# Layer 0 of a two-layer graph kernel: unnormalised row weights, sums inside the owner product, division on ScalarE

## The chip, the core and the metric

The kernel runs on one core of a Trainium2 chip. The metric is the device time of one execution in microseconds. The profile is one profiled execution of the same program; its span and the median of the timed runs differ a little, and both are given below.

Engines: PE (TensorE) multiplies matrices into PSUM, DVE (VectorE) and ACT (ScalarE) work element by element, POOL (GpSimd) issues the indirect DMAs that gather rows, SP issues most other DMAs. Each engine works through its own queue in the order written.

## The reference

`x` is 4096 x 512, `adj` a 4096 x 4096 integer matrix with about 0.1% ones. Layer 0 is graph attention with 8 heads of 64; layer 1 averages the neighbours and mixes them with the node's own row. Each layer is added to its input and normalised.

```python
Wh = einsum('nf,hfo->hno', x, W)
f1 = einsum('hno,ho->hn', Wh, a[:, :F_OUT])
f2 = einsum('hno,ho->hn', Wh, a[:, F_OUT:])
e = leaky_relu(f1[:, :, None] + f2[:, None, :], 0.2)
attn = softmax(where(adj > 0, e, NEG_INF), axis=-1)
x = layernorm(x + concat_heads(attn @ Wh))          # layer 0
agg = mask @ x / max(deg, 1)
nb_f, self_f = agg @ W_nb + b_nb, x @ W_self + b_self
x = layernorm(x + relu(concat(self_f, nb_f) @ W_comb + b_comb))   # layer 1
```

## The kernel before

The 4096 nodes are 32 blocks of 128. The kernel keeps no dense matrix: it turns each row of `adj` into a short list of neighbour indices and gathers rows.

*List stage.* Each adjacency half block is loaded (L391), turned to bf16 on ScalarE (L397), folded by small matmuls (L415) into keys, of which DVE takes maxima (L430). Once for every four blocks `decode` (L432, a generator that yields between its pieces; `some(lists)` advances it by one piece) turns the keys into `lst` (up to 16 indices a node). A node's first `K0` = 3 neighbours have slots of their own; further ones go into `KH` = 2 shared slots of 128 rows for the block, each row with an owner. `own` (one byte each) holds for every shared slot the matrix "row r belongs to node c", `of` the transposed form. At the same time node rows `x @ [W | W a]` are computed (L343) and stored as table `t0`, rows of 8 head scores and 512 values. The last four blocks' lists (28 to 31) are decoded after the last load, between 238 and 257 us.

*Layer 0 loop* (L999 to L1061). Iteration i does parts of several blocks: it gathers block i+4, weighs i+2, sums i+1, normalises i and multiplies block i-1 for layer 1. `gather` (L601) issues five indirect DMAs on POOL, one for each slot, into one of five buffers `g`. For block b:

- `a_weights` (L627): scores e = leaky_relu(f2 gathered + f1), 128 x 5 x 8, on DVE; `a_exp` (L634) on ScalarE.
- `a_shared_sum` (L640): owner matrix times the shared slots' exponentials on PE; `a_sum` (L649 to L653) adds the three own slots and takes the reciprocal, on DVE.
- `a_reach` (L659): PE takes the reciprocal to the shared slots with the transposed owner matrix `st`, which ScalarE casts from `of` (L625). `a_normed` (L667, L670) multiplies the exponentials on DVE.
- `a_weigh` (L674) multiplies the gathered rows by the weights, in place; `a_adds` (L696, L698) adds the three own slots; `a_x` (L682) copies x into PSUM on ScalarE and `a_shared` (L686) adds the owner matrix times the shared rows onto it: two matmuls of 512 columns.
- `a_moments` (L702) on DVE adds both parts and takes the row sum; `root` (L709 to L715) and `norm` (L718) on ScalarE normalise; `transposed` (L322 on PE, copy L328 on ScalarE) and `a_z` (L723 on PE, copy L727) make layer 1's neighbour product, stored as table `t1`.

`fold_weights` (L273) multiplies W_nb by W_comb in sixteen matmuls (L281); it runs in the entry to the loop, between the list pieces. `fold_bias` (L297, line L300) adds four DVE instructions in iterations 2 to 5 and 16 to 19, `sum_bias` one product in iteration 20.

*Layer 1* (L1067 to L1141) gathers from `t1`. The first six blocks' gathers are split: early ones (L608) may start before `t1` is complete, in the buffers that layer 0 gives up; late ones (L611) fetch the rest. Per block it runs `g_self` (L755), `g_shared` (L762), moments and norm.

PSUM is one pool with fixed names: `sm` and `nm` and `pw` two banks each, `key` and `tp` one. A wait between instructions is a semaphore; the order of work is the order in the source, since the schedule is manual.

Of the kernel before, what the change touches and what calls it, by code (L numbers as in the profile page):

```python
# [31 lines left out]
F32 = mybir.dt.float32  # L32
# [8 lines left out]
P = 128  # L41
# [16 lines left out]
LE = 26  # L58
LX = 31
G = 4  # L60
FMAX = 30.0
SHIFT = 136 * 512


@with_exitstack
# [25 lines left out]
def listed_layers(  # L91
# [40 lines left out]
    xt = tc.dram_tile([N, FIN], F32, name="xt")  # L132

    const = ctx.enter_context(tc.tile_pool(name="const", bufs=1))
    ps = ctx.enter_context(tc.tile_pool(name="ps", bufs=1, space=PSUM))
    small = ctx.enter_context(tc.tile_pool(name="small", bufs=3))

    nc.scalar.preload_act_table_set("natural_log_exp_and_others")
# [134 lines left out]
    def fold_weights(loaded, place):  # L273

        wr, wc = loaded
        wT = turned(wr, 0, place(0))
        for c in range(FB):
            nxt = turned(wr, c + 1, place(c + 1)) if c + 1 < FB else None
            mp = ps.tile([P, HD], F32, name="tp", bufs=1)
            for d in range(FB):  # L280
                nc.tensor.matmul(  # L281
                    mp, lhsT=wT[:, d, :], rhs=wc[:, d, :], start=(d == 0), stop=(d == FB - 1)
                )
                if d == FB - 1:
                    nc.scalar.copy(wr[:, c, :], mp)  # L285
                yield
            wT = nxt
# [144 lines left out]
    def decode(b0, dp, place):  # L432
# [60 lines left out]
        for g in range(G):  # L493
            for k in range(KH):
# [1 line left out]
                    pe[:, g, k, :], lhsT=sts[g][:, ts(k, P)], rhs=lst[:, b0 + g, K0:],  # L496
                    start=True, stop=True,
                )
        for g in range(G):
            nc.scalar.copy(of[:, b0 + g, :], sts[g])  # L500
        nc.vector.tensor_copy(es[:, bs], pe[:, :, :, 0:EX])
        nc.vector.tensor_copy(f1s[:, bs, K0:KS, :], pe[:, :, :, EX:])
        kx = dp.tile([P, G, KH], F32, name="kx", bufs=1)
# [104 lines left out]
    def gather_early(b, pool):  # L608
        return gather(t1[0 : 2 + min(LE + b, LX) * P, :], b, pool, idxe)
# [2 lines left out]
        rows_of(gl[:, b, :], t1[:, :], idxl[:, b : b + 1])  # L612


    G0, OWN, ST, E, DN, PR, Y, NM, MV, RS = ({} for _ in range(10))

    def a_owners(b, wp):
        OWN[b] = wp.tile([P, KH, P], F32, name="own", bufs=4)
        nc.scalar.copy(
            OWN[b].rearrange("p k c -> p (k c)"), own[:, b].rearrange("p k c -> p (k c)")  # L620
        )

    def a_owned(b, wp):
        ST[b] = wp.tile([P, KH, P], F32, name="st", bufs=2)
        nc.scalar.copy(ST[b].rearrange("p k c -> p (k c)"), of[:, b, :])  # L625

    def a_weights(b, wp):  # L627
        gw = G0[b][:, :, 0:H]
        e = E[b] = wp.tile([P, KS, H], F32, name="e", bufs=3)
        nc.vector.tensor_add(e, gw, f1s[:, b])  # L630
        nc.vector.scalar_tensor_tensor(e, e, SLOPE, e, OP.mult, OP.max)

    def a_exp(b):
        nc.scalar.activation(E[b], E[b], AF.Exp)  # L634

    def a_shared_sum(b):

        DN[b] = ps.tile([P, H], F32, name="sm", bufs=2)
        for k in range(KH):
            nc.tensor.matmul(  # L640
                DN[b], lhsT=OWN[b][:, k, :], rhs=E[b][:, K0 + k, :],
                start=(k == 0), stop=(k == KH - 1),
            )

    def a_sum(b, wp):

        pd = DN[b]
        dn = DN[b] = wp.tile([P, H], F32, name="dn", bufs=2)
        nc.vector.tensor_reduce(  # L649
            dn, E[b][:, 0:K0, :].rearrange("p k h -> p h k"), AX.X, OP.add  # L650
        )
        nc.vector.tensor_add(dn, dn, pd)
        nc.vector.reciprocal(dn, dn)  # L653

    def a_reach(b):

        PR[b] = ps.tile([P, KH, H], F32, name="sm", bufs=2)
        for k in range(KH):
            nc.tensor.matmul(  # L659
                PR[b][:, k, :], lhsT=ST[b][:, k, :], rhs=DN[b], start=True, stop=True  # L660
            )

    def a_normed(b):

        e = E[b]
        w = E[b] = ps.tile([P, KS, H], F32, name="key", bufs=1)
        nc.vector.tensor_tensor(  # L667
            w[:, 0:K0, :], e[:, 0:K0, :], DN[b].unsqueeze(1).to_broadcast([P, K0, H]), OP.mult
        )
        nc.vector.tensor_mul(w[:, K0:KS, :], e[:, K0:KS, :], PR[b])  # L670

    def a_weigh(b, sl, to=None):
        gv = G0[b][:, sl, H:TW].rearrange("p k (h d) -> p k h d", h=H)
        nc.vector.tensor_tensor(  # L674
            gv if to is None else to.rearrange("p (k h d) -> p k h d", k=1, h=H), gv,
            E[b][:, sl].unsqueeze(3).to_broadcast([P, sl.stop - sl.start, H, D]), OP.mult,
        )

    def a_x(b):

        NM[b] = ps.tile([P, HD], F32, name="nm", bufs=2)
        nc.scalar.copy(NM[b], xs[:, b, :])  # L682

    def a_shared(b):
        for k in range(KH):
            nc.tensor.matmul(  # L686
                NM[b], lhsT=OWN[b][:, k, :], rhs=G0[b][:, K0 + k, H:TW],
                start=False, stop=(k == KH - 1), skip_group_check=True,
            )

    def a_adds(b, wp):

        yp = ps.tile([P, HD], F32, name="pw", bufs=2)
        a_weigh(b, slice(0, 1), yp)
        a_weigh(b, slice(1, K0))
        nc.vector.tensor_add(yp, yp, G0[b][:, 1, H:TW])  # L696
        Y[b] = wp.tile([P, HD], F32, name="y", bufs=2)
        nc.vector.tensor_add(Y[b], yp, G0[b][:, 2, H:TW])  # L698

    def a_moments(b):  # L700
        mu = MV[b] = small.tile([P, 1], F32, name="ln_sum")
        nc.vector.scalar_tensor_tensor(  # L702
            Y[b], Y[b], 1.0, NM[b], OP.mult, OP.add, accum_out=mu
        )

    def root(b, wide):
# [88 lines left out]
    def some(todo):  # L795
        for p in todo:
            next(p, None)
# [9 lines left out]

    oo_cm = tc.tile_pool(name="owners", bufs=1, side="right")
    oo = oo_cm.__enter__()
    of = oo.tile([P, NB, KH * P], U8, name="of")  # L810
    own = oo.tile([P, NB, KH, P], U8, name="own8")
    dp_cm = tc.tile_pool(name="decode", bufs=1, side="right")
    dp = dp_cm.__enter__()
# [84 lines left out]
        return wp.tile([P, KH * P], F32, name="own", bufs=4)  # L898

    def on_last(b):  # L900
        if b % 2 == 0:
            last[0] = wp.tile([P, FB, P], F32, name="xT", bufs=2)
        return last[0].rearrange("p (g k) r -> p g (k r)", g=2)[:, b % 2, :]

    last = {}

    def store(w, row, eng=nc.scalar):
        eng.dma_start(t0[2 + w * P : 2 + (w + 1) * P, :], row[:, 0:TW])
# [65 lines left out]
        return wp.tile([P, FW], F32, name="row", bufs=2)[:, 0:FIN]  # L974

    m2s = fold_weights(loaded, place)
    a_owners(0, wp)
    a_owned(0, wq)
    for k in range(7):
        some(lists)  # L980
    for k in range(4):
        next(m2s)
    lists = [decode(NB - G, dp, on_last)]
    for k in range(8):
        some(lists)
    for k in range(3):
        next(m2s)
    for k in range(3):
        some(lists)
    for k in range(2):  # L990
        next(m2s)


    def on(b):
        return 0 <= b < NB

    XT, G1 = {}, {}
    biased = fold_bias(loaded, bcol[:, FB:])
    for i in range(-2, NB + 1):  # L999
        if on(i):  # L1000
            a_moments(i)
        if on(i - 1 + GA):
            G0[i - 1 + GA] = gather(t0, i - 1 + GA, gps[(i - 1 + GA) % GA])
        elif i > 0:
            b = i - 1 + GA - NB
            G1[b] = gather_early(b, gps[(NB + b) % GA])
        if on(i + 1):
            a_reach(i + 1)
        if i == -1:
            for k in range(2):  # L1010
                next(m2s)
        if i >= -1 and on(i + 2):
            a_owned(i + 2, wq)
        if on(i + 1):
            a_x(i + 1)
            a_normed(i + 1)
            a_weigh(i + 1, slice(K0, KS))
        if on(i + 2):
            a_weights(i + 2, wq)
        if on(i):  # L1020
            root(i, xs[:, i, :])
        if on(i + 2):
            a_exp(i + 2)
        for k in range({-2: 3}.get(i, 0)):
            some(lists)
        if on(i):
            norm(i, xs[:, i, :])
        if on(i - 1):
            a_z(i - 1, XT.pop(i - 1), m2, wp)
        if on(i + 1):  # L1030
            a_adds(i + 1, wq)
        if i == 0:
            a_shared_sum(i + 2)
            a_shared(i + 1)
        if on(i):
            XT[i] = transposed(i, wp)
            store_xT(i, XT[i])
        if on(i + 2):
            if i:
                a_shared_sum(i + 2)  # L1040
            for k in range({-2: 1}.get(i, 0)):
                some(lists)
            a_sum(i + 2, wq)
            for k in range({-2: 1}.get(i, 0)):
                some(lists)
        for k in range({-2: 3, -1: 2}.get(i, 0)):
            next(m2s)
        if on(i + 1) and i:
            a_shared(i + 1)
        if on(i + 3):  # L1050
            a_owners(i + 3, wp)
        if 2 <= i < 6:
            next(biased)
        if i == 7:
            loaded = load_fold(0, w_self, m1, weight(fc, "wc"))
        if 16 <= i < 20:
            if i == 16:
                biased = fold_bias(loaded, bcol[:, 0:FB])
            next(biased)
        if i == 20:  # L1060
            sum_bias()  # L1061


    dp_cm.__exit__(None, None, None)
    oo_cm.__exit__(None, None, None)
# [74 lines left out]
            nc.vector.tensor_add(flag, fl[:, 0:1], fl[:, 1:2])  # L1140
    g_norm(NB - 1, wp)  # L1141
    fc_cm.__exit__(None, None, None)


@with_exitstack
# [391 lines left out]
```

## Time and profile before

| | us |
|---|---|
| median of 3 runs (691.61 to 692.17) | 691.87 |
| span of the profiled execution | 691.2 |
| list stage, to the last adjacency load's landing | 0 to 226.4 |
| block 0's normalisation starts (first L709) | 265.03 |
| block 31's normalisation starts | 481.84 |
| last `a_z` copy ends | 490.2 |
| last PE instruction ends | 677.9 |

Busy time by stage, from the windows view (us; the granted TensorE clock as a share of full speed):

| window | length | PE | DVE | ACT | POOL | clock |
|---|---|---|---|---|---|---|
| 228.0 to 262.0, entry | 34.0 | 29.59 | 25.88 | 9.63 | 26.04 | 0.73 |
| 262.0 to 282.4 | 20.4 | 17.68 | 14.23 | 10.66 | 13.63 | 0.75 |
| 282.4 to 317.5 | 35.1 | 34.18 | 32.57 | 24.71 | 23.93 | 1.00 |
| 317.5 to 481.8 | 164.3 | 161.87 | 147.29 | 114.55 | 110.99 | 1.00 |
| 481.8 to 502.0, exit | 20.2 | 17.41 | 7.00 | 8.56 | 15.05 | 1.00 |

How to read it: the busy share of an engine is only meaningful within a stage. "Spacing" below is the distance from the start of one instruction to the start of the next on the same engine; it is less than the duration where instructions overlap, and more where one waits. PEld is the weight load of PE, which overlaps its matmuls. A row such as `L723 x8` stands for four matmuls of float32, of which each leaves two records.

### The profile page before, as it was taken

The page shows a single profiled execution, that of the slowest core. Times are in us where ns is not written, and L with a number is a line of the kernel's source. Part 1 is how long each engine was busy: PE and PEld are TensorE (multiplying, and loading weights), DVE is VectorE, ACT ScalarE, POOL GpSimd, SP SyncE. Part 2 cuts the span into 40 slices and gives each one's busy share as a digit, 9 for nine tenths or more (in the row PEclk, how much of TensorE's full clock was granted, in tenths as well). Part 3 has the DMA queues.
Part 4 walks back from the last instruction along what each step waited for, and adds up shares of the span by engine and source line. Part 5 has one row for each costly group of instructions (what it writes and reads, how often), then busy time and mean ns, then how long its engine had stood idle before and what let it go on. Part 6 is the DMA issues. An engine that isn't in the chain of part 4 may idle for free.

```text
span 691.2 us, 9191 instructions
## 1 busy us (share of the span) xinstructions
PE 626.3 (91%) x2354; PEld 345.0 (50%) x2354; DVE 498.4 (72%) x1431; ACT 455.6 (66%) x1044; POOL 348.0 (50%) x410
## 2 busy tenths in 40 slices
PE   4688998897798698999999999999899999999993
PEld 2466766665565444545455444554344444444441
DVE  6246996998787878799988998898304656666663
ACT  3677988888777434667677767776316567767764
POOL 4001111010011677677676776747776677777760
PEclk9999999999999587999999999999999999999997
DMA  8999999999899877788989888968978889998991
GB/s 259 404 408 408 410 407 408 407 408 409 322 325 334 275 196 214 226 265 270 381 274 282 262 263 265 279 215 272 298 206 268 277 300 308 316 304 298 329 308 70
DMA packets 92038, 209.65 MB, mean 303 GB/s; under 512 B 13694, under 2 KB 13702, under 8 KB 91978
## 3 DMA queue, kind: packets, MB, share of 16 engines
q1 hardware_dynamic: 63024, 114.05, 44.6%
q0 software_dynamic: 28624, 94.39, 43.9%
q10 hardware_dynamic: 330, 0.54, 0.2%
q8 instruction: 21, 0.34, 0.2%
q14 instruction: 39, 0.32, 0.1%
HBM read 175.25 MB, written 33.69 MB: 302 GB/s over the span
## 4 chain that ended last, share of the span: by engine, by line
PE 60%; DVE 14%; DMA 14%; ACT 4%; issue 4%; POOL 2%; SPq 1%; DVEq 0%; ACTq 0%; POOLq 0%
PE pw L723 12%; DMA at<-in_adj_dram 11%; PE nm L755 8%; PE pw L755 8%; PE nm L686 7%; PE pw L343 5%; PE nm L762 4%; PE pw L762 4%; PE tp L281 3%; ACT ab L397 3%; POOL g L592 2%; PE tp L322 2%; PE sm L659 2%; DMA g<-t,idx 2%; PE sm L640 1%
## 5 line engine op out<-in xcount | busy, mean ns | idle before, releaser
L592 POOL DMA_INDIRECT g<-t,idx x290 | 280.6, 968 | 116.4 <-issue 49.7
L397 ACT ACTIVATE ab<-at 128x2048 bf16<-128x2048 int32 x64 | 122.2, 1913 | 33.3 <-DMA at<-in_adj_dram 28.0
L343 PE MATMUL pw<-w_sb,xT 128*128 128x264 f32 x512 | 133.3, 407 | 10.7 <-DVE sums L332 4.7
L723 PE MATMUL pw<-wr,xT 128*128 128x512 f32 x256 | 119.7, 611 | 1.4 <-ACT xT L328 1.3
L343 PEld LDWEIGHTS pw<-w_sb,xT 128*128 128x128 f32 x512 | 96.2, 197 | 39.6 <-issue 7.3
L354 POOL COPY f1s<-lst 128x24 f32<-128x24 f32 x32 | 7.3, 229 | 180.8 <-DVE fmax L351 96.4
L674 DVE TENSOR_TENSOR g<-g,key 128x1024 f32<-128x1024 f32 x64 | 77.8, 1216 | 1.1
L723 PEld LDWEIGHTS pw<-wr,xT 128*128 128x128 f32 x256 | 47.0, 194 | 49.3 <-issue 47.5
L686 PE MATMUL nm<-g,own 128*128 128x512 f32 x128 | 64.5, 627 | 0.0
L755 PE MATMUL nm<-m,xT 128*128 128x512 f32 x128 | 57.5, 592 | 0.0
L755 PE MATMUL pw<-m,xT 128*128 128x512 f32 x128 | 57.5, 592 | 0.0
L778 DVE SCALAR_TENSOR_TENSOR sm<-y,lst,nm 128x512 f32<-128x512 f32 x16 | 12.1, 755 | 52.8 <-PE nm L772 29.2
L709 ACT ACTIVATE xs<-y,ln_sum 128x512 f32<-128x512 f32 x32 | 23.1, 722 | 39.2 <-DVE y L702 39.2
L322 PEld LDWEIGHTS tp<-ident,xs 128*128 128x128 f32 x256 | 30.2, 147 | 36.3 <-ACT xs L718 18.4
L322 PE MATMUL tp<-ident,xs 128*128 128x128 f32 x256 | 41.7, 287 | 7.4 <-DVE sums L332 7.1
L347 DVE COPY row<-pw 128x264 f32<-128x264 f32 x64 | 26.9, 422 | 19.4 <-PE pw L343 14.6
L755 PEld LDWEIGHTS pw<-m,xT 128*128 128x128 f32 x128 | 24.3, 190 | 30.6 <-issue 30.4
L755 PEld LDWEIGHTS nm<-m,xT 128*128 128x128 f32 x128 | 24.3, 190 | 30.6 <-issue 30.6
L592 POOL DMA_INDIRECT g<-t,idxe x30 | 28.4, 947 | 16.8 <-issue 6.7
L281 PE MATMUL tp<-wc,row 128*128 128x512 f32 x64 | 34.1, 676 | 2.0 <-ACT m L285 1.2
L762 PE MATMUL nm<-g,own 128*128 128x512 f32 x64 | 30.2, 594 | 1.2 <-ACT nm L746 1.2
L686 PEld LDWEIGHTS nm<-g,own 128*128 128x128 f32 x128 | 22.5, 196 | 16.3 <-issue 15.9
(213 smaller groups left out, 1072.8 us busy)
## 6 DMA issues: line engine op xcount, KB each, us to landing
at<-in_adj_dram SPq DMA_DIRECT2D x64, 1024.0 KB, 10.7
xt<-xT SPq DMA_DIRECT2D x32, 256.0 KB, 4.1
t<-row SPq DMA_DIRECT2D x32, 256.0 KB, 3.9
xT<-xt SPq DMA_DIRECT2D x32, 256.0 KB, 4.9
out_dram<-row SPq DMA_DIRECT2D x32, 256.0 KB, 5.2
t<-row POOLq DMA_DIRECT2D x31, 260.0 KB, 5.5
xs<-in_x_dram SPq DMA_DIRECT2D x31, 256.0 KB, 10.9
g<-t,idx POOLq DMA_INDIRECT x290, 4.8
```

The lines of the kernel that those rows point to most:

```text
L281: nc.tensor.matmul(mp, lhsT=wT[:, d, :], rhs=wc[:, d, :], start=(d == 0), stop=(d == FB - 1))
L322: nc.tensor.transpose(tp[:, c, :], xs[:, b, ts(c, P)], ident)
L343: nc.tensor.matmul(pw, lhsT=xT[:, c, :], rhs=w_sb[:, c, k * HW : (k + 1) * HW], start=(c == 0), stop=(c == FB - 1),)
L347: nc.vector.tensor_copy(row[:, k * HW : (k + 1) * HW], pw)
L397: nc.scalar.activation(ab, loads.pop((b, h)), AF.Relu, accum_out=asum[:, b, h : h + 1])
L592: nc.gpsimd.indirect_dma_start(out=out, out_offset=None, in_=table, in_offset=bass.IndirectOffsetOnAxis(ap=at, axis=0),)
L674: nc.vector.tensor_tensor(gv if to is None else to.rearrange("p (k h d) -> p k h d", k=1, h=H), gv, E[b][:, sl].unsqueeze(3).to_broadcast( ...
L686: nc.tensor.matmul(NM[b], lhsT=OWN[b][:, k, :], rhs=G0[b][:, K0 + k, H:TW], start=False, stop=(k == KH - 1), skip_group_check=True,)
L709: nc.scalar.activation(wide, Y[b], AF.Square, bias=MV[b], scale=-float(HD), accum_out=rs)
L723: nc.tensor.matmul(pz, lhsT=xT[:, c, :], rhs=m2[:, c, :], start=(c == 0), stop=(c == FB - 1))
L755: nc.tensor.matmul(NM[b], lhsT=xT[:, c, :], rhs=m1[:, c, :], start=False, stop=(c == FB - 1), skip_group_check=True,)
L762: nc.tensor.matmul(NM[b], lhsT=OWN[b][:, k, :], rhs=g[:, K0 + k, 0:HD], start=False, stop=(k == KH - 1), skip_group_check=True,)
```

## The change

The weights are no longer normalised before they are used. Rows are weighed by plain exponentials; the exponentials of the shared slots are written into the gathered rows, in front of the values (columns 0 to 7), so that the owner product sums weights and values together, and each node's sum is divided out at the end, head by head, by eight ScalarE instructions (`a_scale`). `a_shared_sum`, `a_sum`, `a_reach`, `a_normed`, `a_owned`, `a_x` and the store `of` go. The product for a block, `num`, is 8 sums and 512 values, kept in two banks: 264 columns and 256. The three own slots are weighed and added straight into `num` on DVE before the owner product adds to it; x is added in `a_moments`.

The loop is one step deeper: iteration i weighs i+3, sums i+2, multiplies owners and divides i+1, normalises i. `a_owners` and the gather move ahead accordingly (gather of i+6). Block 2 is gathered before the loop. The last four blocks' lists are decoded one piece an iteration, over iterations -3 to 12; `last` is a buffer of its own for them. PSUM is laid out anew for the loop and again after it (class `Banks`), with four matmuls that fill the two `num` tiles once. `FMAX`, the bound on head scores above which the dense path would be taken, goes from 30 to 20.

```diff
-FMAX = 30.0
+FMAX = 20.0
+class Banks:
+    def stage(self, bufs, names=None):
+        self.close()
+        self.n += 1
+        self.cm = self.tc.tile_pool(name=f"ps{self.n}", bufs=1, space=PSUM)
+        self.pool = self.cm.__enter__()
+        self.bufs, self.names = bufs, names or {}
+    def tile(self, shape, dtype, name, bufs=None):
+        name = self.names.get(name, name)
+        return self.pool.tile(shape, dtype, name=name, bufs=self.bufs[name])
...
-        for g in range(G):
-            nc.scalar.copy(of[:, b0 + g, :], sts[g])
...
     def a_exp(b):
-        nc.scalar.activation(E[b], E[b], AF.Exp)
-    def a_shared_sum(b):
-    def a_sum(b, wp):
-    def a_reach(b):
-    def a_normed(b):
+        e = E[b]
+        w = E[b] = ps.tile([P, KS, H], F32, name="ew")
+        nc.scalar.activation(w, e, AF.Exp)
+        nc.scalar.activation(G0[b][:, K0:KS, 0:H], e[:, K0:KS, :], AF.Exp)
+    def halves_of(t):
+        return t[:, H : H + 2 * (2 * HH - H)].rearrange(
+            "p (a c) -> p a c", a=2
+        )[:, :, 0:HH]
+    def a_first(b):
+        NM[b] = ps.tile([P, 2 * HD], F32, name="num")
+        nc.vector.tensor_tensor(
+            halves_of(NM[b]).rearrange("p a (h d) -> p a h d", d=D),
+            G0[b][:, 0, H:TW].rearrange("p (a h d) -> p a h d", a=2, d=D),
+            E[b][:, 0].rearrange("p (a h) -> p a h", a=2).unsqueeze(3).to_broadcast(
+                [P, 2, H // 2, D]
+            ),
+            OP.mult,
+        )
+    def a_own_sum(b):
+        nc.vector.tensor_reduce(
+            NM[b][:, 0:H], E[b][:, 0:K0, :].rearrange("p k h -> p h k"), AX.X, OP.add
+        )
+    def a_adds(b):
+        for k in range(1, K0):
+            nc.vector.tensor_add(
+                halves_of(NM[b]), halves_of(NM[b]),
+                G0[b][:, k, H:TW].rearrange("p (a c) -> p a c", a=2),
+            )
     def a_shared(b):
-        for k in range(KH):
-            nc.tensor.matmul(
-                NM[b], lhsT=OWN[b][:, k, :], rhs=G0[b][:, K0 + k, H:TW],
-                start=False, stop=(k == KH - 1), skip_group_check=True,
-            )
+        for a in range(2):
+            r = slice(a * (H + HH), H + HH + a * HH)
+            for k in range(KH):
+                nc.tensor.matmul(
+                    NM[b][:, a * HD : a * HD + r.stop - r.start],
+                    lhsT=OWN[b][:, k, :], rhs=G0[b][:, K0 + k, r],
+                    start=False, stop=(k == KH - 1), skip_group_check=True,
+                )
+    def a_recip(b, wp):
+        RD[b] = wp.tile([P, H], F32, name="rd", bufs=2)
+        nc.vector.reciprocal(RD[b], NM[b][:, 0:H])
+    def a_scale(b):
+        Y[b] = ps.tile([P, HD], F32, name="yp")
+        for h in range(H):
+            a, q = divmod(h, H // 2)
+            o = a * HD + (1 - a) * H + q * D
+            nc.scalar.mul(
+                Y[b][:, h * D : (h + 1) * D], NM[b][:, o : o + D], RD[b][:, h : h + 1]
+            )
-    def a_moments(b):
+    def a_moments(b, wp):
+        yp = Y[b]
+        Y[b] = wp.tile([P, HD], F32, name="y", bufs=2)
...
-            Y[b], Y[b], 1.0, NM[b], OP.mult, OP.add, accum_out=mu
+            Y[b], yp, 1.0, xs[:, b, :], OP.mult, OP.add, accum_out=mu
...
+    ps.stage(
+        dict(num=2, ew=1, yp=1, tp=1, pw=1), dict(key="yp", sm="tp", mp="pw")
+    )
+    for k in range(2):
+        t = ps.tile([P, 2 * HD], F32, name="num")
+        for a in range(2):
+            nc.tensor.matmul(
+                t[:, a * HD : (a + 1) * HD], lhsT=triu, rhs=cols, start=True, stop=True
+            )
+    G0[2] = gather(t0, 2, gps[2])
...
-    for i in range(-2, NB + 1):
+    for i in range(-3, NB + 2):
+        if on(i + 1):
+            a_shared(i + 1)
+        if on(i + 1 + GA):
+            G0[i + 1 + GA] = gather(t0, i + 1 + GA, gps[(i + 1 + GA) % GA])
+        elif on(i + GA - NB - 1) and i + GA - NB - 1 < GA:
+            b = i + GA - NB - 1
+            G1[b] = gather_early(b, gps[(NB + b) % GA])
+        if on(i + 3):
+            a_weights(i + 3, wq)
+        if on(i + 2):
+            a_weigh(i + 2, slice(K0, KS))
+        if on(i + 1):
+            a_recip(i + 1, wq)
+        if on(i + 2):
+            a_first(i + 2)
+            a_weigh(i + 2, slice(1, K0))
+            a_own_sum(i + 2)
+            a_adds(i + 2)
+        if on(i):
+            root(i, xs[:, i, :])
+            norm(i, xs[:, i, :])
+        if on(i + 1):
+            a_scale(i + 1)
+        some(lists)
+        if on(i + 1):
+            a_moments(i + 1, wq)
+        if on(i + 3):
+            a_exp(i + 3)
+        for k in range({-3: 3, -2: 2, -1: 2}.get(i, 0)):
+            next(m2s)
+        if on(i + 4) or i == -3:
+            a_owners(i + 4, wp)
+        if on(i - 1):
+            a_z(i - 1, XT.pop(i - 1), m2, wp)
+        if on(i):
+            XT[i] = transposed(i, wp)
+            store_xT(i, XT[i])
...
+    ps.stage(dict(nm=2, pw=2, sm=2, key=1, tp=1), dict(mp="tp"))
```

## The prediction

> **What bounds the kernel now.** The page first, then windows by stage, the chain of waits and the timeline of one iteration. The run has three stages: lists from the adjacency matrix (0 to 226 us), layer 0 (to 490 us), layer 1. Page, windows (length; busy us of PE, PEld, DVE, ACT, POOL, instructions in brackets; granted clock, DMA share, GB/s), chain (start, length), and ScalarE's timeline:
>
> ```profile
> PE 626.3 (91%) x2354; PEld 345.0 (50%) x2354; DVE 498.4 (72%) x1431; ACT 455.6 (66%) x1044; POOL 348.0 (50%) x410
> ...
> 268.00:270.00 2.00, 2.00 (x5) 0.97 (x5) 1.93 (x3) 0.00 (x0) 1.48 (x2) 0.50 0.78 210
> ...
> 317.50:481.80 164.30, 161.87 (x573) 82.80 (x573) 147.29 (x335) 114.55 (x307) 110.99 (x117) 1.00 0.87 277
> ...
> 317.48 3.54 PE pw L723 x8
> 321.80 1.82 PE nm L686 x4
> 323.96 3.54 PE pw L723 x8
> ...
> 282.40 0.72 ACT L709 ACTIVATE xs<-y,ln_sum 128x512 f32<-128x512 f32 x1 [1.16 <-DVE y L702]
> ...
> 330.95 0.72 ACT L709 ACTIVATE xs<-y,ln_sum 128x512 f32<-128x512 f32 x1 [1.21 <-DVE y L702]
> 331.58 0.19 ACT L709 ACTIVATION_READ_ACCUMULATOR xs<-y,ln_sum 128x1 f32 x1
> 331.80 0.29 ACT L712 ACTIVATE ln_rs<-ln_rs,eps 128x1 f32<-128x1 f32 x1
> 332.13 0.20 ACT L713 ACTIVATE ln_rs<-ln_rs 128x1 f32<-128x1 f32 x1
> 332.24 0.19 ACT L714 ACTIVATE ln_sum<-ln_sum 128x1 f32<-128x1 f32 x1
> 332.45 0.29 ACT L715 ACTIVATE ln_sum<-ln_sum,ln_rs 128x1 f32<-128x1 f32 x1
> 332.94 0.24 ACT L634 ACTIVATE e<-e 128x40 f32<-128x40 f32 x1 [0.19 <-DVE e L631]
> 333.08 0.80 ACT L718 ACTIVATE xs<-y,ln_sum,ln_rs 128x512 f32<-128x512 f32 x1
> 334.49 0.58 ACT L727 COPY row<-pw 128x512 f32<-128x512 f32 x1 [0.60 <-PE pw L723]
> 334.97 0.59 ACT L328 COPY xT<-tp 128x512 f32<-128x512 f32 x1
> 335.45 0.42 ACT L619 CAST own<-own 128x256 f32<-128x256 uint8 x1
> 335.75 0.41 ACT L625 CAST st<-of 128x256 f32<-128x256 uint8 x1
> 336.06 0.60 ACT L682 COPY nm<-xs 128x512 f32<-128x512 f32 x1
> ...
> 481.84 0.72 ACT L709 ACTIVATE xs<-y,ln_sum 128x512 f32<-128x512 f32 x1 [1.81 <-DVE y L702]
> ```
>
> The loop's stage has PE at 161.9 of 164.3 us and DVE at 147.3, tied through L653, L659, L670 and L702; ScalarE has 30% free. From block 2's L709 (282.40) to block 31's (481.84) are 199.4 us, 29 steps of 6.88. The 268 line shows half clock in the entry.
>
> **What the Trainium skill says.** "ScalarE: Activation LUTs", section "What ACT_TABLE_LOAD costs": an ACTIVATE with immediates takes 186 ns + 0.833 per element, each per-partition pointer 93 more, neighbours overlap by 93. The trace agrees: 187 ns (L714), 294 with one pointer (L715), 802 for 512 elements with two (L718); L625 starts 0.30 us after a 0.42 us cast. Same page, section "Step-by-step: what each stage is for": ScalarE writes PSUM sooner than SBUF; L736, SBUF to PSUM, is 578 ns where the formula gives 613. "TensorE: Matmul & The Clock Gate", Part 1: half clock after about 3.4 us of idling, until as much sustained work. Here PE idled 2.7 us before L640 at 267.24; then L723 took 5.62 us instead of 3.68.
>
> **The change part by part.** (1) PE, per block. The sums L640 and reaches L659 go: in the chain of waits 0.35 and 0.34 us. The owner product becomes four matmuls of 264 or 256 columns: L343's 264-column form issues eight rows in 1.79 us against L686's 1.82. PE is left with 3.54 (L723) + 0.5 (transposes) + 1.8 = 5.9 us.
>
> (2) DVE, per block. Its spacing without waits is 6.57 us (L670's successor at 324.77 to that at 331.34). L652, L667 and L670 go, 0.20 + 0.29 + 0.22; the other widths stay. About 5.8. The moments now also wait for ScalarE's divisions. Queued behind them are the next weights; from those to the last add I sum starts of the same rows: 0.37 + 1.14 + 0.15 + 0.60 + 1.14 + 0.20 + 0.80 + 0.70 = 5.1.
>
> (3) ScalarE, per block: the cast `st` (0.30 spacing) and copy of x (0.49) go; a second small exp comes (0.12), and eight scalings of 128x64, PSUM to PSUM, by a pointer. The order of instructions shows that seven of them wait on ScalarE itself, so they can't overlap. No row is this operation. From above: 186 + 53 + 93 = 332 ns by the formula, plus 0.03 (end of L712 to L713), 0.37 apart. From below: no wait felt, 0.25 apart. PSUM ends cost less: L335, 128x128 from PSUM, is 273 ns with its accumulator, leaving 166 fixed, and L736 leaves 151. I take 166 - 20 + 53 + 100 = 300 ns, 0.33 apart. Eight, up to the next exp's start: 7 x 0.33 + 0.30 - 0.09 = 2.52.
>
> The iteration by starts, in its new order: square 0.63, read 0.22, Ln 0.33, exp 0.11, mul 0.21, mul 0.32, normalise 0.71, scalings 2.52, exps 0.26, owners 0.30, two copies 0.98: 6.6; the same rows of before add up to 4.74 where the windows show 114.55/164.3 x 6.88 = 4.80, so I add 0.06: 6.65. That makes ScalarE the longest cycle. Does anything stretch it? Take block i's square as 0. Block i+1's divisions run from 2.6 to 5.2; before them stands the new wait for DVE's reciprocal, with both exps, the owners' cast and two copies queued behind it, but the reciprocal follows only weights and the weighing of two rows on DVE (0.37 + 1.14 after the moments) and the owner product of the step before, so it is ready near 0.9. DVE's moments of i+1 take 5.2 to 5.9, ahead of their square at 6.65. DVE's next series ends 5.1 later, at 4.3 of the next cycle, 0.9 before its moments can start; then the owner product runs 4.3 to 6.1. L723 waits for the copy of the transposes, at 0.1, and ends at 3.7, the transposes at 4.2; their copy on ScalarE comes at 6.2. Nothing is late, so 6.65 stands.
>
> (4) POOL. Five gathers a block at 1.25 apart are 6.26 us, below the cycle. Buffers are freed in the order first, add, add, owner product, and refilled three iterations before use: nothing.
>
> (5) The last lists. They occupy DVE from 238.5 to 256.4 in the entry; now one of 16 steps an iteration, beside DVE's slack of 0.8 us. Most steps are 0.7 to 1.3 us. The one at 244.9 (1.5) and the one with the products at 253.25 (1.5 plus 1.7 of PE) spill: 1.5 us in all, and the bias copy at block 20 adds 0.3 on ScalarE. Sum 1.8.
>
> (6) Entry. Decoding of lists 24 to 27 now waits for the four bank-filling matmuls behind MAX8 at 230.5: 2.2 us later. The foldings (four groups of 3.5 to 6 us with copies between) still stand ahead: the first owner product after 14 instead of 16 of 16, near 257 against 262.3. One more pipeline step and DVE's in-order queue (3.5 us of block 1, a decode step of 1, moments 0.7) put block 0's square at 264.7, as before (265.03). Block 1's follows 6.6 later, 271.2 instead of 274.4. PE idles there, so I leave half of a cold product's loss (5.6 - 3.7): block 2's at 279.2 instead of 282.40. Gain 3.2; between -2, colder for longer, and 5.5, no cold step.
>
> (7) List stage. 28 `of` casts go; ScalarE waited 2.35 to 3.5 us for transposes after them and the adjacency loads carry the stage: nothing. FMAX 20: the largest projected score of the given inputs is 11.6, so the dense path stays out.
>
> (8) Exit. From block 31's square to the last product's copy 8.3 us in both. POOL's early gathers begin later against that end (shorter last iterations, one owner product later in the queue); their 30 x 1.25 us were continuous until the late ones at 496.75. I see 1.6 us more lag, and the last gather landed (670.7 + 4.8) only 0.7 before its product (676.2): loss 1, between 0 and 3.
>
> Sum: the loop is 29 x 6.65 + 1.8 = 194.7 against 199.4, gain 4.7; entry 3.2; exit -1. Together 6.9 off the span of 691.2, 684.3; the median of the runs is 0.7 above the span, so 685.0.
>
> **Rivals.** *Divisions dearer, slower than before*: place ScalarE's loop. At 0.39 apart (a PSUM read and write in one instruction costing more than either) the cycle is 6.65 + 7 x 0.06 = 7.07, the loop 206.8: 691.2 + 7.4 - 3.2 + 0.5 = 695.9, so 696.6. It decides above 0.365 apart, where 29 cycles eat all gains (6.89). For: no row shows such an instruction, and the formula taken literally gives 0.365. Against: the PSUM rows are shorter. *Divisions cheap*: at 0.25 apart the cycle would be 6.1, POOL's 6.26 with its release waits takes over near 6.35: 186.0 for the loop, gain 13.4 + 3.2 - 1, 676.3. For: independent neighbours overlap. Against: the waits. *Entry lost*: the extra pipeline step and a cold PE take 2 instead of giving 3.2: 690.2. For: 2.7 us idle sufficed before. Against: the decode steps no longer stand before block 0.
>
> **How the numbers follow.** Forecast 0.48 (own range 681 to 689), dearer 0.23, cheap 0.17, entry lost 0.12. A measurement here tells 0.2%, 1.4 us, from no change: faster 0.48 + 0.17 + 0.10, same 0.03, slower 0.22. The range runs from mid-cheap, 676.5, to near the dearer case, 695.
>
> **What would show it.** Right: L713's scalings near 300 ns and 0.33 apart, ScalarE at 95% of the loop, PE falling below 90%, the squares 6.6 to 6.7 apart, block 2's at 279. Wrong: scalings over 0.365 apart; squares waiting for DVE's moments; POOL without idle time between gathers; PE at half clock beyond block 2.

## The result and the profile after

| | before | after |
|---|---|---|
| median, us (runs; lowest to highest) | 692.02 (4; 691.61 to 692.23) | 685.07 (4; 681.32 to 687.94) |
| span of the profiled execution | 691.2 | 679.5 |
| block 2's normalisation starts | 282.40 | 278.25 |
| block 31's normalisation starts | 481.84 | 469.34 |
| last `a_z` copy ends | 490.18 | 478.70 |
| last PE instruction ends | 679.6 | 668.2 |

(The 677.9 given further up for the last row is too early; the trace has 679.6.)

The ratio is 0.9898, with a 95% interval of 0.9861 to 0.9935: 7 us faster. The runs of the kernel after spread over 6.6 us where those of before spread over 0.6, and the profiled one is the fastest of them, so its span gains 11.7 us.

The experiments below come from three later comparisons, whose kernels have names with `e`, `r` and `p`, and from one kernel compared alone, `x_chain`. In the three comparisons all kernels, the one before too, took close to 800 us, and in every trace of them the engines stood still for 2 to 4 us about every third block of the loop, for no reason that the trace names. There the kernel before has a few quick runs among many slow ones, so that the medians put the changed kernel 7.8 and 3.3 us ahead, while the quickest runs put it 12.0 and 7.1 us behind (795.60 against 783.57, 792.79 against 785.65), and three variants in the third comparison came out 0.4 to 1.2% behind by the quick runs. So the 7 us are shown by the first comparison; the later ones don't confirm them. From their traces only stretches between the standstills are read. `x_chain`, 686.93 us beside 690.79 of before, is free of them.

The page of the kernel after, its first line of busy times and two of its groups (busy us, mean ns of one, idle time before them):

```profile
PE 598.6 (88%) x2230; PEld 341.7 (50%) x2230; DVE 478.3 (70%) x1335; ACT 488.0 (72%) x1236; POOL 345.8 (51%) x410
...
L742 PE MATMUL pw<-wr,xT 128*128 128x512 f32 x256 | 118.1, 604 | 6.1 <-ACT xT L351 5.9
L713 ACT ACTIVATE yp<-num,rd 128x64 f32<-128x64 f32 x256 | 73.1, 286 | 11.2 <-DVE rd L705 3.8
```

ScalarE's timeline of one free iteration of the kernel after (start, length, operation):

```profile
318.36 0.74 ACT L728 ACTIVATE xs<-y,ln_sum 128x512 f32<-128x512 f32 x1
...
320.21 0.82 ACT L737 ACTIVATE xs<-y,ln_sum,ln_rs 128x512 f32<-128x512 f32 x1
320.93 2.51 ACT L713 ACTIVATE yp<-num,rd 128x64 f32<-128x64 f32 x8
323.36 0.20 ACT L653 ACTIVATE ew<-e 128x40 f32<-128x40 f32 x1
323.49 0.20 ACT L654 ACTIVATE g<-e 128x16 f32<-128x16 f32 x1
323.59 0.39 ACT L640 CAST own<-own 128x256 f32<-128x256 uint8 x1
323.89 0.58 ACT L746 COPY row<-pw 128x512 f32<-128x512 f32 x1
324.37 0.59 ACT L351 COPY xT<-tp 128x512 f32<-128x512 f32 x1
324.84 0.74 ACT L728 ACTIVATE xs<-y,ln_sum 128x512 f32<-128x512 f32 x1
```

No line carries an idle time in brackets: ScalarE, which waited three times in the iteration shown of before, waits for nothing now, and the squares (L728, the first instruction of a block's normalisation) are 324.84 - 318.36 = 6.48 us apart. Such a distance is called a step below, and a free step where nothing stands still in it. The division row takes 2.43 us to the next exponential, 37% of the step. In L713's instructions seven of each eight carry a wait for the one ahead of them on ScalarE. Two windows of the kernel after (columns: length; busy us of PE, PEld, DVE, ACT and POOL; granted clock, DMA share, GB/s):

```profile
352.00:397.00 45.00, 41.50 (x141) 23.55 (x140) 40.55 (x82) 42.48 (x140) 34.34 (x36) 1.00 0.92 288
397.00:413.00 16.00, 13.68 (x42) 8.09 (x41) 11.62 (x23) 13.40 (x43) 10.22 (x12) 0.89 0.78 245
```

In the first, ScalarE is the busiest engine and PE, at 98% before, has fallen to 92%. The second is the stretch of the bias sum, with a clock of 0.89.

All squares together: from block 2 to 31 are 191.1 us. 29 x 6.48 are 187.9. On top come 1.8 + 0.9 at the bias sum (steps of 8.29 and 7.35), 1.1 where DVE has a piece of the last decode and a row of `fold_bias` to do (7.60, with 1.5 and 0.7 us on DVE) and 0.6 in three other steps; the last three steps, without exponentials and casts, are 1.2 shorter together.

The exit, PE's timeline of the kernel after:

```profile
469.52 3.70 PE L742 MATMUL pw<-wr,xT 128*128 128x512 f32 x8 [1.81 <-ACT xT L351]
473.06 0.60 PE L345 MATMUL tp<-ident,xs 128*128 128x128 f32 x4
474.38 3.70 PE L742 MATMUL pw<-wr,xT 128*128 128x512 f32 x8 [0.73 <-ACT xT L351]
```

Block 31 is normalised by 472.0 (L737 at 471.19 for 0.82), but its transposes stand behind block 30's product until 473.06. From its square to the last copy are 9.36 us, against 8.34 before. After that the 11.5 us stay whole to the end of layer 1.

### The profile page after: what moved, and what is told of

Read it like the earlier page. It is cut to its first block, busy times and chain, and to the rows that moved or that the text cites. A ratio compares the mean times of both kernels' runs of the same rounds, so it can differ in the third digit from the quotient of the medians.

```text
span 679.5 us, 8946 instructions
## 1 busy us (share of the span) xinstructions
PE 598.6 (88%) x2230; PEld 341.7 (50%) x2230; DVE 478.3 (70%) x1335; ACT 488.0 (72%) x1236; POOL 345.8 (51%) x410
## 4 chain that ended last, share of the span: by engine, by line
PE 36%; ACT 18%; DVE 6%; issue 3%; DMA 2%; POOL 1%; ACTq 0%; DVEq 0%; POOLq 0%
PE pw L774 8%; PE nm L774 8%; ACT yp L713 5%; PE nm L781 4%; PE pw L781 4%; PE pw L742 3%; ACT xs L737 2%; PE tp L304 2%; PE pw L304 2%; ACT xs L728 2%; DVE g L663 2%; PE num L697 2%; ACT xT L351 2%; ACT row L746 1%; DVE num L687 1%
## 5 line engine op out<-in xcount | busy, mean ns | idle before, releaser
L366 PE MATMUL pw<-w_sb,xT 128*128 128x264 f32 x512 | 132.4, 405 | 11.2 <-DVE sums L355 5.1
L742 PE MATMUL pw<-wr,xT 128*128 128x512 f32 x256 | 118.1, 604 | 6.1 <-ACT xT L351 5.9
L663 DVE TENSOR_TENSOR g<-g,ew 128x1024 f32<-128x1024 f32 x64 | 77.5, 1211 | 7.7 <-ACT ew L653 7.7
L713 ACT ACTIVATE yp<-num,rd 128x64 f32<-128x64 f32 x256 | 73.1, 286 | 11.2 <-DVE rd L705 3.8
L697 PE MATMUL num<-g,own 128*128 128x264 f32 (+1 forms) x256 | 67.2, 408 | 10.0 <-DVE num L687 6.5
L697 PEld LDWEIGHTS num<-g,own 128*128 128x128 f32 x256 | 48.2, 198 | 23.0 <-DVE num L687 10.7
L345 PEld LDWEIGHTS tp<-ident,xs 128*128 128x128 f32 x256 | 31.2, 145 | 34.2 <-issue 11.5
L687 DVE TENSOR_TENSOR num<-num,g 128x512 f32<-128x512 f32 x64 | 44.8, 699 | 2.2
L721 DVE SCALAR_TENSOR_TENSOR y<-yp,xs 128x512 f32<-128x512 f32 x32 | 21.9, 686 | 15.7 <-ACT yp L713 15.5
```

The lines of the kernel that those rows point to most:

```text
L345: nc.tensor.transpose(tp[:, c, :], xs[:, b, ts(c, P)], ident)
L366: nc.tensor.matmul(pw, lhsT=xT[:, c, :], rhs=w_sb[:, c, k * HW : (k + 1) * HW], start=(c == 0), stop=(c == FB - 1),)
L663: nc.vector.tensor_tensor(gv, gv, E[b][:, sl].unsqueeze(3).to_broadcast([P, sl.stop - sl.start, H, D]), OP.mult,)
L687: nc.vector.tensor_add(halves_of(NM[b]), halves_of(NM[b]), G0[b][:, k, H:TW].rearrange("p (a c) -> p a c", a=2),)
L697: nc.tensor.matmul(NM[b][:, a * HD : a * HD + r.stop - r.start], lhsT=OWN[b][:, k, :], rhs=G0[b][:, K0 + k, r], start=False, stop=(k == KH ...
L713: nc.scalar.mul(Y[b][:, h * D : (h + 1) * D], NM[b][:, o : o + D], RD[b][:, h : h + 1])
```

## The experiments

### What sets the step of 6.48 us

The divisions into an SBUF tile instead of a PSUM bank (`e2_sbuf`, `r_sbuf`, `p_sbuf`; the same kernel three times):

```diff
-        Y[b] = ps.tile([P, HD], F32, name="yp")
+        Y[b] = wp.tile([P, HD], F32, name="y", bufs=2)
...
-        yp = Y[b]
-        Y[b] = wp.tile([P, HD], F32, name="y", bufs=2)
...
-            Y[b], yp, 1.0, xs[:, b, :], OP.mult, OP.add, accum_out=mu
+            Y[b], Y[b], 1.0, xs[:, b, :], OP.mult, OP.add, accum_out=mu
```

In the instructions this does one thing more: into one PSUM bank, seven of the eight divisions wait for the one ahead of them on ScalarE; into separate columns of SBUF none does. The waits stand in the program as it was built; whether the chip needs them in PSUM is not shown.

> The eight divisions write an SBUF tile instead of a PSUM bank, and the moments work in place there; then none of the eight waits for the one before. Theory A: ScalarE is the loop's bound (6.48 us a step, of which the divisions 2.43 at 0.316 apart). Without the waits they should stand about 0.22 apart, 1.8 us together, ScalarE would need 5.85, and the step falls to the next bound, near 6.3 (POOL's five gathers are 6.26): 29 steps x 0.18, some 5 us off. Rival B: the step is set by the chain through DVE's moments or by PE, and ScalarE only looks full: the same time within 1.5 us.

> One part of the change alone: the eight divisions write an SBUF tile, and the moments sum into it in place; nothing is left out. Theory A (the row of divisions on ScalarE, 2.43 us from the first to the next exponential, sets the free step of 6.48 us): the row takes about 1.8 us and the free step falls by 0.6 us or more, to 5.6 to 5.9; over 29 steps 17 to 25 us if nothing else is slower, so a time of 660 to 668. Theory B (the gathers on GpSimd, five at 1.25 us a block, are the floor): the free step stays at or above 6.26, and the time falls by 6 us at most.

> The divisions into SBUF, which don't wait for one another (1.57 us for the row in place of 2.43), nothing else changed. Between disturbances of the earlier runs the free step was then 5.62 us, but never for more than three steps together, so that the gathers on GpSimd could catch up. Theory A (ScalarE's row alone sets the step): 5.6 to 5.7 us over the whole loop, 22 to 25 us less than the changed kernel, 658 to 665 us. Theory B (below 6.26 us the five gathers of 1.25 us set it): 5.6 for the first blocks at most, then 6.26 to 6.35 with VectorE or GpSimd named as what the gathered rows wait for; 4 to 7 us less, 678 to 681 us.

Times: 796.56 beside 805.31 of before, 796.79 beside 803.31, 800.8 beside 804.77. They decide nothing. ScalarE's timeline of `r_sbuf` between two standstills, from normalisation to normalisation:

```profile
486.77 0.81 ACT L735 ACTIVATE xs<-y,ln_sum,ln_rs 128x512 f32<-128x512 f32 x1
487.49 1.73 ACT L713 ACTIVATE y<-num,rd 128x64 f32<-128x64 f32 x8
489.06 0.25 ACT L653 ACTIVATE ew<-e 128x40 f32<-128x40 f32 x1
...
490.81 0.74 ACT L726 ACTIVATE xs<-y,ln_sum 128x512 f32<-128x512 f32 x1
...
496.43 0.78 ACT L726 ACTIVATE xs<-y,ln_sum 128x512 f32<-128x512 f32 x1
```

The row is 489.06 - 487.49 = 1.57 us, as in most iterations of all the kernels of this form, and the step 5.62 (5.61 to 5.67 wherever nothing disturbs it). Row and step are shorter by the same 0.86 us. Theory A's mechanism holds: the step follows ScalarE's row one for one. That five gathers of 1.25 us keep the *single* step above 6.26 falls. Whether they would over a whole loop is not decided: while gathers run, steps of 5.6 us stand singly, and after a standstill in which the gathers caught up; the step shown comes after the last gather of this layer, with POOL idle from 482 to 493 us, and the five in a row at the end of `p_all` stand there too. PE (3.44 + 0.43 + 1.76 by starts) and DVE have no gap over 0.1 us in that step either, so below 5.62 two more limits follow at once.

Is it PSUM or the wait? `x_chain` keeps SBUF and brings six of the waits back: six divisions write one column more, over which the next one writes.

```diff
+            w = D + (q < H // 2 - 1)
             nc.scalar.mul(
-                Y[b][:, h * D : (h + 1) * D], NM[b][:, o : o + D], RD[b][:, h : h + 1]
+                Y[b][:, h * D : h * D + w], NM[b][:, o : o + w], RD[b][:, h : h + 1]
```

> The divisions into SBUF as before, but six of the eight write one column more, which the next division writes over, so that each of six waits for the one ahead of it, as all do in the changed kernel; nothing is left out. In stretches without other waits the changed kernel's divisions began 0.316 us apart (2.43 us from the first to the next exponential) and those into SBUF without waits 0.20 apart (1.57). Theory A (the wait on the instruction ahead makes the difference): 0.29 to 0.33 us apart where there is a wait, 2.15 to 2.3 from the first division to the next exponential, free step 6.2 to 6.35. Theory B (writing to PSUM makes it): about 1.6 and a free step of 5.6 to 5.7, as without waits.

686.93 us beside 690.79 of before (one run of each), span 685.1. ScalarE's timeline of it:

```profile
358.47 0.81 ACT L736 ACTIVATE xs<-y,ln_sum,ln_rs 128x512 f32<-128x512 f32 x1
359.19 2.59 ACT L714 ACTIVATE y<-num,rd 128x65 f32<-128x65 f32 x8
361.68 0.20 ACT L653 ACTIVATE ew<-e 128x40 f32<-128x40 f32 x1
...
363.16 0.74 ACT L727 ACTIVATE xs<-y,ln_sum 128x512 f32<-128x512 f32 x1
```

The row is 2.49 us and the free step 6.53: longer than the changed kernel's 2.43 and 6.48, with one wait fewer. One row holds both kinds: the six pairs with a wait start 0.33 to 0.35 us apart, the one pair without (between the two halves) 0.21, with the same source and destination memories. So the wait, with the signal that goes with it, is the cost: 0.15 us each into SBUF (0.92 / 6). For PSUM 0.86 / 7 gives 0.12, if a row without waits took 1.57 us there too, which no run shows. Theory A had the sign and B falls, but my size for it (2.15 to 2.3) was too low. The Trainium skill, "Perfetto Trace Analysis", section "Optimizing Scalar/DVE Operations", offers a reason: part of a profiled instruction is its write acknowledgement, which overlaps with the next one, and the overhead is larger on SBUF than on PSUM. A wait for the instruction ahead would take that overlap away. The trace agrees in kind: without waits a division of 0.32 us is followed after 0.20, with one after 0.35. That the acknowledgement is what is waited for, no run shows by itself.

### What the bias sum costs

PE's timeline of the kernel after at the bias sum (`L331`):

```profile
400.34 0.60 PE L345 MATMUL tp<-ident,xs 128*128 128x128 f32 x4
403.26 1.12 PE L331 MATMUL tp<-brow,ones 128*128 128x512 f32 x2 [2.32 <-ACT xT L351]
404.22 3.57 PE L697 MATMUL num<-g,own 128*128 128x264 f32 x8
407.58 3.67 PE L742 MATMUL pw<-wr,xT 128*128 128x512 f32 x8
```

The new bank plan gives `sm` and `tp` one bank. The bias product, written right after the transposes, has to wait until ScalarE has copied them, 2.3 us, and the next block's owner product waits behind it on PE, some 3.4 us late in all, and runs at half clock, 3.57 us in place of 1.92.

In `e3_bias`, `r_lists` and `p_lists` the sum stands one iteration later, behind the owner product; the latter two also decode the last lists in the entry, as `e4_entry` does alone (of the edit below the first two pieces move the lists, the last two the sum):

```diff
     lists = [decode(NB - G, dp, on_last)]
+    for k in range(16):
+        some(lists)
...
-        some(lists)
         if on(i + 1):
             a_moments(i + 1, wq)
...
+        if i == 21:
+            sum_bias()
         if on(i - 1):
             a_z(i - 1, XT.pop(i - 1), m2, wp)
...
-        if i == 20:
-            sum_bias()
```

> The product that sums the bias rows moves from the end of iteration 20 to iteration 21, between the owner product and the layer 1 product, which waits for the same copy anyway. Theory A: the two steps of 8.29 and 7.35 us at 397 to 412 us come from PE waiting 2.3 us for that copy at the head of its queue, with the half clock that follows; they become about 6.5 to 7, 2 to 2.7 us off. Rival B: the half clock there has another cause, and the time stays.

> The last lists are decoded in the entry again (all 16 pieces before the loop), everything else as in the changed kernel. Theory A: the entry's gain hangs on this: DVE is taken from about 241 to 258 us before block 0 is weighed, block 0's square moves from 264.2 to about 269, and the loop gets back about 1.5 us of steps that the pieces lengthened: 3 to 4 us slower than the changed kernel. Rival B: the foldings on PE hold the entry alone: no change or 1.5 us faster.

> Two parts of the change alone: the sum of the bias is issued one iteration later, behind the owner product and ahead of the last product, and all pieces of the last decode stand in the entry, ahead of the last five pieces of the folding; nothing is left out. Theory A (what the sum of the bias costs is that the owner product stands behind it on TensorE until the copy of the transposes has freed the bank): the two steps of 8.29 and 7.35 become 6.5 to 7.6 each, 1.5 to 2.5 us less together; the step of 7.60 at the row lists becomes 6.48, and the first squares come 0 to 1 us later; together 2 to 3 us off, 682 to 683 at the median. Theory B (the extra half clock comes from how little TensorE does in the loop, wherever the bias is summed): the half clock comes all the same and the two steps keep 15 us together.

> The sum of the bias one iteration later, behind the owner product, and the last decode's sixteen pieces in the entry; divisions as in the changed kernel; nothing left out. Theory A (the owner product stood behind the bias product and its bank): the two steps of 8.29 and 7.35 us are 13.0 to 14.2 together, no half clock there; the steps of 7.60, 6.82 and 6.64 become 6.48; the entry is 0 to 2 us longer; 681 to 683.5 us at the median. Theory B (half clock comes whenever the loop is that thin): 15 us or more for the two steps, and a time of 684 us or more.

The times (798.36, 796.28, 802.0, 801.55) again decide nothing. PE's timeline of `p_lists`:

```profile
447.21 0.60 PE L345 MATMUL tp<-ident,xs 128*128 128x128 f32 x4
447.65 1.95 PE L697 MATMUL num<-g,own 128*128 128x264 f32 x8
449.43 1.08 PE L331 MATMUL tp<-brow,ones 128*128 128x512 f32 x2
450.35 3.60 PE L742 MATMUL pw<-wr,xT 128*128 128x512 f32 x8
```

The owner product follows the transposes, and the bias product starts without a wait: theory A's mechanism. The gain is not shown. The step there is 6.48, but the one after it holds a standstill, 10.34 like others without a bias sum. In it the next transposes wait for the bias row's copy, 2.46 us in `p_lists` and 0.85 in `r_lists`: the bank is still shared, so the new place is not free either. In `r_lists` the two steps are 6.92 and 11.79. In `e3_bias` they are 8.81 and 7.42, no better than before: ScalarE stood still 2.1 us after the owner product, and PE waited 2.02 us for the copy in the new place too, half clock following. `e4_entry`, with the sum where it was, has a step of 8.29 and then 6.47, PE waiting 1.58 us for the copy and no half clock. So does `x_chain`, with 8.34 and then 6.53:

```profile
409.06 1.12 PE L331 MATMUL tp<-brow,ones 128*128 128x512 f32 x2 [2.39 <-ACT xT L351]
410.02 1.92 PE L697 MATMUL num<-g,own 128*128 128x264 f32 x8
```

Where it stands, the sum costs 1.8 us, three times over, of which its own copy on ScalarE (L332) is 0.5. The half clock after it, 0.9 us more in the profiled run, comes or doesn't with nearly the same idle time (2.32 us there, 2.39 here), so theory B, half clock wherever the loop is thin, doesn't hold as it was put. The traces show what makes the difference. In all fourteen the granted clock changes only on a grid of 3.41 us, which lies differently in each execution. PE in two windows of this grid, of the kernel after and then of `x_chain` (length; busy us; granted clock, DMA share, GB/s):

```profile
400.91:404.32 3.41, 1.09 (x4) 1.00 0.80 226
404.32:407.74 3.42, 3.42 (x10) 0.50 0.93 333
...
405.08:408.50 3.42, 1.59 (x7) 1.00 0.91 293
408.50:411.91 3.41, 2.85 (x11) 1.00 0.91 285
```

In the first the idle time falls into one window, PE is busy for 32% of it, and the next window is at half clock. In `x_chain` it is spread over two, 46% and 84% busy, and the clock stays. Counted over all traces from 60 to 670 us: each of the 165 windows at full clock with PE busy for less than 41% was followed by half clock, and of the 1884 with 48% or more only 10, for reasons that stay open; between these shares it was 19 of 42.

What the list pieces cost in the loop or the entry, the standstills in the entries hide (block 0's square comes at 276.8 to 288.7 us in the traces of the three comparisons, in no order that follows the edit); `e4_entry` is inconclusive.

### Both edits, and the spread

> The edits of the two kernels before together. Theory A: both gains add up, 657 to 666 us, with TensorE the busiest engine of the loop. Theory B (GpSimd is the floor): within 1 us of the kernel with the moved list work alone, plus 6 us of gain at most.

> Both edits together. Theory A: the gains add up, 655 to 663 us. Theory B (gathers of 6.26 us a block under both): 674 to 679 us, and the moved list work still saves its 2 to 3 us, since the gathers too waited for those blocks.

`r_all` took 797.24 beside 803.31 of before, `p_all` 802.68 beside 804.77. Both have free steps of 5.62 us, and still three blocks with a standstill take 23.41 us in `p_all` (320.30 to 343.71) and 23.41 in the changed kernel's repeat `r_after` (319.47 to 342.88). Shorter steps only made the standstills longer, 11.2 instead of 10.4 us for the block that held one. From block 2 to block 30 the traced loops took 207.9 to 219.4 us with free steps of 5.62 and 208.8 to 213.6 with 6.48. So the gain of a faster step could not be seen in any total, and no version is shown here to beat the changed kernel.

> The changed kernel as it is, for its spread (681.3 to 687.9 us in four runs, where the kernel before spans 0.6). Theory A: the spread is time at TensorE's half clock, which starts at a different place in each execution, so runs with a lower mean clock are longer, and the extra time stands in the entry to the loop (228 to 278 us) or at the bias product (404 us), while the free steps of the loop stay at 6.48 us in every profile. Rival B: the loop's own step varies, by gathers that come late. Then steps between 305 and 400 us would differ from 6.48.

> The changed kernel as it is, as the measure for the other three. Most steps of the loop 6.48 us from square to square, with two longer ones (8.29 and 7.35) at the sum of the bias and one (7.60) where the last decode forms its row lists. What is asked of it: the four runs so far lay between 681.3 and 687.9 us with mean TensorE clocks of 0.963 and 0.953. Theory A says that the spread comes from one or two more stretches at half clock in the loop or the entry, of which each costs 1.5 to 3 us; theory B says that it comes from the list stage before 228 us, the same in both kernels.

The two repeats (797.56 and 800.03) had free steps of 6.48 again, but couldn't tell where the spread of 681 to 688 comes from. A lead came from `x_chain`, where two steps were 9.28 and 9.87 us. Its timeline, lines of ScalarE and PE:

```profile
338.29 0.58 ACT L745 COPY row<-pw 128x512 f32<-128x512 f32 x1 [1.66 <-DMA t<-row]
...
339.74 0.58 ACT L351 COPY xT<-tp 128x512 f32<-128x512 f32 x1 [0.87 <-DMA xt<-xT]
...
340.38 0.93 PEld L518 LDWEIGHTS tp<-lst,last 128*128 128x128 f32 x4 [3.52 <-ACT xT L351]
```

At iteration 7 the layer 1 weights are loaded, 2 MB, on the queue that also stores `row` and `xT`, and DMA runs at 393 to 406 GB/s from 330 to 340. The `xT` store issued next behind them landed 15.1 us after its issue (324.55 to 339.67), where others take 4 to 5; in the profiled run of the changed kernel that store took 12.6. A `row` buffer was not stored in time, then an `xT` buffer; ScalarE waited 2.5 us, PE 3.1, and then PE ran at half clock until about 347 (granted clock 0.50 from 342 to 346). There the same steps were 6.82 and 6.64, so the meeting cost it 0.5 us and this one 6.1. Those 5.6 us more are the 5.6 between the two spans, since the other differences nearly cancel: 29 x 0.05 for the longer row, against 0.9 for the half clock that did not come at the bias sum and 0.8 for a quicker entry (block 2 at 277.47). The slower runs of the changed kernel were not traced, so what made them slow is not shown. Their mean clock, 0.953 against 0.963 in the two quicker ones, stands for about 14 us more at half clock (an estimate, 0.010 x 686 / 0.5); `x_chain` at 0.960 has about 4, so this one meeting alone would not explain them. (The kernel before waited 1.7 us for a `row` store in this stretch as well.)

## Why the prediction was right, and where not

The predicted 685.0 us meets the median of 685.07, and the reason given, ScalarE as the new longest cycle because its divisions wait for one another, is what the runs show. One of its signs of being wrong did come, PE at half clock beyond block 2, at the bias sum, and cost 0.9 us. That the numbers meet so closely is partly chance: against its own profile the prediction gave 6.9 us of gain in the span, and the profiled run had 11.7, while the other runs lost up to 6.6 of them again.

1. *PE left with 5.9 us a block*: right in kind; by starts it is 5.62, which shows once the divisions are shorter.
2. *DVE 5.8, not in the way*: right. DVE waits for the divisions in most iterations; it fits into 5.62.
3. *ScalarE 6.65, divisions 300 ns, 0.33 apart, 2.52 together*: mechanism right, size 0.17 a step too high. Measured: 286 ns, 0.318, 2.43 and 6.48. Half of the excess was the row, half the other rows with their added 0.06. Over 29 steps 4.9 us. "ScalarE: Activation LUTs", section "What ACT_TABLE_LOAD costs", gives an estimate of 332 ns; into SBUF the trace has 324, into PSUM 286, so the shorter PSUM ends were rightly taken off. What a wait for the instruction ahead costs is not in that section, and it decides: some 0.12 us a time.
4. *POOL nothing*: right for this kernel, whose step lies above 6.26.
5. *Last lists 1.8*: lists 1.5 put, 1.2 measured (the steps of 7.60 and 6.62). The bias sum, put at 0.3 as a copy on ScalarE, was mis-sized by most: 2.7 measured, 0.5 the copy itself, 1.3 the waits that come with its place, 0.9 the half clock. The late stores, 0.5 (6.82 and 6.64), had no term. I had not followed its PSUM name through the new bank plan, nor asked what stood behind it on PE.
6. *Entry 3.2*: block 0's square at 264.16 (put at 264.7), block 1's at 270.44 (271.2), block 2's at 278.25 (279.2): 4.15. PE's half clock came, with 3.81 and 4.55 us for two products that take 1.92 and 3.60 later; the step that holds it was 7.81, put at 8.0. Which part of the change brought the entry forward is not shown, since `e4_entry` could not decide it.
7. *List stage nothing*: right, its loads carry it.
8. *Exit -1, by POOL's lag*: -1.0, but on PE: the last transposes behind block 30's product. The early gathers were not what the end waited for; late ones began 9.35 us sooner, at 487.40 against 496.75.

The loop's sum was 4.7 us of gain and became 8.3: 4.9 from the shorter step and 1.2 from the three last steps, which I had counted as full ones, less 2.6 at the bias sum, the lists and the late stores. The dearer divisions, my rival on the other side, needed 0.365 us apart; `x_chain`, with its waits in SBUF, comes to 0.35 and shows how near that was. The cheap rival's spacing is real too, 0.20, if the eight write where nothing makes them wait.

## What to carry to other kernels

Look in the instruction list whether small instructions on one engine wait for the one ahead, before taking their price from other rows: here the same division started 0.20 us after the last one without a wait and 0.32 to 0.35 with it. If they write separate parts, try a destination in which they count as separate. When a bank plan changes, follow every name that was put onto a shared bank to its last user, also those that run once: here it was not the one product that cost, but the long row that queued behind it. And look which large load falls into a loop: here a store behind 2 MB of weights landed 12 to 15 us after its issue in place of 4 to 5.

## What the runs showed that was not expected

- The same eight divisions take 1.57, 2.43 or 2.49 us, by the wait and the memory alone.
- Half clock is not set by the length of an idle time alone: "TensorE: Matmul & The Clock Gate", Part 1, has it after about 3.4 us of idling, but 2.32 us brought it in one run and 2.39 us at the same place did not in another; 3.12 us, at the late stores, did. What fitted in these traces was how little PE did within one window of the 3.41 us grid.
- With standstills of 2 to 4 us, three blocks often took 23.4 us whatever the kernel's step, 6.48 or 5.62. They tend to come at fixed places: `e4_entry`, `r_lists`, `p_lists` and `p_all` each have one before the same three instructions of PE (numbers 2566, 2692 and 2902 of its recorded list, weight loads and waits counted). That points to the program's order rather than to chance, but `r_sbuf` and `p_sbuf`, the same kernel, share only some places. It is not the chip alone: chip 11 gave both 797 us (`e1_again`) and 687 (`x_chain`). What stands still there, the trace doesn't name: in `p_lists` ScalarE and VectorE waited after an owner product that by the profile had ended at 408.8, and the record of the wait says no more than this:

```profile
411.84 0.59 ACT L746 COPY row<-pw 128x512 f32<-128x512 f32 x1 [3.85 <-remote]
412.02 0.21 DVE L705 RECIPROCAL rd<-num 128x8 f32<-128x8 f32 x1 [2.37 <-remote]
```
